# An attention transform that works in PSUM, shifted copies in parts, and another order for the stages beside it

## The chip, the cores and the metric

One core of a Trainium2 chip runs the whole program. The metric is the device time of one execution in microseconds (us). Before the change the median of three executions is 7252.11 us (7241.76 to 7254.39). The profiled execution has a span of 7245.1 us at a mean granted TensorE clock of 0.845.

## What is computed

Two layers on four images `x[4, 96, 128, 128]`, all in float32. Layer 0 is a selective-scan block; it isn't touched except for its last step, which is called norm here: layer norm over 192 channels, a projection to 96 channels and the residual. Layer 1, which the change concerns, is for each image:

```python
# xr, x1, x2: a "split norm" of the group-normed image: parts above and below the mean
x1 = sc1 * relu(x) + x1n;   x2 = sc2 * (x - relu(x)) + x2n
key, qry = unfold(conv2d(x1, aw1), 3), unfold(conv2d(x2, aw2), 3)
attn = softmax(einsum('bckl,bqkl->bqck', key, qry) / sqrt(C * 9))      # [96, 96 * 9]
value = conv2d(x1, aw3)
y1 = layer_norm(conv2d(value, attn as 3x3 weights))
y2 = layer_norm(conv2d(x2, w_conv2)) * x1
out = x + xr + conv1x1(concat(y1, y2), w_full) + b_full
```

All 3x3 convolutions have 96 channels in and out.

## The kernel before

**Convolution as products.** The columns of a row are cut in tiles of four. A tile with its borders (six columns) is turned into six planes by sums and differences (`planes_of`, L1319 and on); the convolution is then six products with transformed weights (`products`, L1371 on), and an output transform makes four columns of the six results (`outputs`, L1438 on). The planes of x1, x2 and value lie in DRAM (`x1p`, `x2p`, `vp`).

`planes_of` has two forms. `at_once` does all on VectorE. `scaled` makes scaled copies x4 and x2 on ScalarE (L1346, L1347), and `differences` makes the planes from them on GpSimd (L1352 to L1358, in the profile df, x and pl).

`products` works on a strip of 12 rows. It takes three pairs of PSUM banks (tile `two`): one pair for products 0 and 5, one for 1 and 3 ("a"), one for 2 and 4 ("b"). Each product sums three matrix products, from `ya` (planes as loaded), from `yb` (the first 64 channels of ya shifted by one and two rows, L1393 both) and from the last 32 channels (L1408). `yb` is made by ScalarE in `turn` (L1797), in two copies of 64x2376, before the products of the strip ahead. `outputs` copies the first pair to SBUF (`ou`, L1456) and pair a (`sd`, L1480) on ScalarE; VectorE makes sums and differences of pair a with pair b (L1464, L1465), adds to `ou` (L1466), and writes the four columns with L1474, each from two SBUF tiles.

**Attention** of one image (`attention`): for each of 11 strips and each of two maps (x1 and x2), one set of products of 128 channels and one of 64 channels on two half strips; beside these the transposes and products that make the attention map (`taps`, L1655 and L1551). Then softmax, and 11 more strips of products over value (`vp`). Image 0 has only these last 11, since its first part is done in another way ahead of this (`direct_maps`, L1948).

**Light work beside it.** `norm` (`ssm_output`, L942 to L1041) makes layer 0's output. `split` (`split_norm`) has a first pass for statistics (L1093 to L1100) and a second pass that makes x1 and x2 (L1196 on ScalarE, L1201 on VectorE, tile `half`) and their planes, 16 pieces of 8 rows with two sides each. `close` (`attn_output`, L2060 to L2076) joins all to the output.

**Order.** All work is written as generators that yield a cost. `co_run` lets the light generator go on as far as the attention generator (left) has paid; when left ends, what is left of light is drained. `Later` holds work back for a number of ticks, so that evacuations are issued between products. An instruction scheduler then orders each engine's queue; a queue runs in order, and DMAs from SP have one queue. The light work goes round in this way (stage b is attention of image b):

```python
    for b in range(NB):
        after = []
        if 0 < b and b + 1 < NB:
            after.append(imgs[b + 1].split(psr, "right"))
        if b:
            imgs[b].begin()
            after.append(imgs[b - 1].close(psr, "right"))
        if b + 2 < NB:
            imgs[b + 2] = Image(b + 2)
            after.append(imgs[b + 2].norm(yms[b // 2 + 1][b % 2], psr, "right"))
        light = chain(*([light] if b == 0 else []), *after)
```

The `light` of stage 0 is what remains of norm and split of image 1. The attention pool `psa` has three pairs of PSUM banks, `psr`, for light work, has two single banks.

## Time and profile before

| Stretch, us | What runs | Length |
|---|---|---|
| 3740 to 3945 | stage 0: image 0's value products, second pass of split of image 1 | 205 |
| 3945 to 4012 | stage 0: rest of that split | 67 |
| 4012 to 4262 | stage 0: norm of image 2 | 250 |
| 4262 to 5370 | stage 1: attention of image 1, with split of image 2 (to 4850), close of image 0 (to 5045), norm of image 3 | 1108 |
| 5370 to 6375 | stage 2: attention of image 2, with split of image 3 (to 5975), close of image 1 (to 6180), then nothing | 1005 |
| 6375 to 7110 | stage 3: attention of image 3, with close of image 2 (to 6585), then nothing | 735 |
| 7110 to 7245 | close of image 3 | 135 |

Before 3740 us lie layer 0's projection and scan and image 0's first part. Over the whole span PE is busy 76%, VectorE 68%, ScalarE 53% and GpSimd 52%; these are means over stages with different limits, so the stages have to be read one by one. In the profile PE is TensorE's matmul, PEld its weight load, DVE is VectorE, ACT ScalarE, POOL GpSimd, and SP the engine that issues most DMAs. In a group of instructions the tile before the arrow is written, those behind it are read; then come the count, the busy time, the mean of one in ns, and the idle time before it with what ended it.

### The profile page before, as it was taken

How to read it: one execution, taken by the hardware profiler on the slowest of the kernel's cores; microseconds unless marked ns; L12 is line 12 of the kernel's file. 1: busy time of each engine (PE TensorE's matmuls, PEld its weight loads, DVE VectorE, ACT ScalarE, POOL GpSimd, SP SyncE). 2: the span in 40 equal slices, each digit the busy share in tenths (PEclk: the TensorE clock that was granted, in tenths of full speed). 3: DMA queues.
4: the chain of work that ended last, by engine and by line, in shares of the span. 5: the costliest groups of instructions: out<-in, count | busy, mean ns of one | idle time of the engine just before them, and what ended most of it. 6: DMA issues, size and time to landing. Idle time of an engine off the chain costs nothing. (4 is left out here: it accounts for less than half of the span.)

```text
span 7245.1 us, 74140 instructions
## 1 busy us (share of the span) xinstructions
PE 5487.0 (76%) x23256; PEld 2382.5 (33%) x23256; DVE 4907.5 (68%) x6580; ACT 3876.0 (53%) x4296; POOL 3731.4 (52%) x2734
## 2 busy tenths in 40 slices
PE   5889989878877289999834565568875668888887
PEld 2333323222221044443311123334333334445542
DVE  3257779888975788895478346558566558676457
ACT  1357677777865766773333254444455444444443
POOL 2237669788874388892123228972217982122310
PEclk9999989989976599999867577779887779889887
DMA  8767777757666667567665553447674436665346
GB/s 145 183 155 192 200 196 211 224 162 211 186 166 187 183 197 218 173 189 190 177 164 155 136 141 98 111 111 186 167 184 105 111 101 178 152 176 131 91 120 171
DMA packets 886276, 1183.96 MB, mean 163 GB/s; under 512 B 208190, under 2 KB 745350, under 8 KB 873404
## 3 DMA queue, kind: packets, MB, share of 16 engines
q1 hardware_dynamic: 862268, 1124.28, 59.1%
q0 software_dynamic: 16208, 38.42, 2.0%
q10 hardware_dynamic: 7408, 16.53, 0.8%
q8 instruction: 186, 3.05, 0.2%
q14 instruction: 206, 1.69, 0.1%
HBM read 771.50 MB, written 337.56 MB: 153 GB/s over the span
## 5 line engine op out<-in xcount | busy, mean ns | idle before, releaser
L621 PE MATMUL bank<-y,wp 128*128 128x512 f32 (+3 forms) x3584 | 1315.4, 623 | 94.9 <-DVE z L497 39.9
L854 POOL TENSOR_TENSOR y<-y,dl 128x1024 f32<-128x1024 f32 x384 | 1057.7, 2754 | 267.4 <-DVE dl L846 233.3
L821 POOL TENSOR_TENSOR dl<-dl,u 128x1024 f32<-128x1024 f32 x384 | 1012.9, 2638 | 223.2 <-ACT dA L797 102.7
L842 DVE TENSOR_TENSOR_SCAN dA<-dA,pBC 128x512 f32<-128x512 f32 x768 | 981.6, 1278 | 30.7
L1393 PE MATMUL two<-ya,wd 128*64 128x192 f32 (+3 forms) x2376 | 622.3, 446 | 330.7 <-ACT sd L1480 219.1
L621 PEld LDWEIGHTS bank<-y,wp 128*128 128x128 f32 (+3 forms) x3584 | 458.6, 169 | 763.2 <-issue 653.0
L1948 PE MATMUL bank<-y,wn 128*128 128x384 f32 (+5 forms) x2408 | 676.4, 504 | 41.6 <-DMA y<-x2d 16.6
L846 DVE TENSOR_TENSOR dl<-dA,pBC 128x512 f32<-128x512 f32 x768 | 528.7, 688 | 262.6 <-PE pBC L735 189.0
L735 PE MATMUL pBC<-xr,wbc 60*128 60x512 bf16 (+1 forms) x1536 | 456.9, 402 | 329.1 <-DVE dA L842 256.1
L1393 PE MATMUL two<-yb,wd 128*64 128x192 f32 (+3 forms) x2376 | 594.2, 427 | 3.7 <-ACT yb L1797 3.7
L664 ACT ACTIVATE dl<-pd,dtb 128x512 f32<-128x512 f32 x768 | 486.2, 684 | 186.9 <-PE pd L735 173.7
L1464 DVE TENSOR_TENSOR sd<-sd,two 128x384 f32<-128x384 f32 (+5 forms) x176 | 137.6, 782 | 586.9 <-ACT sd L1480 577.9
L1797 ACT COPY yb<-ya 64x2376 f32<-64x2376 f32 (+1 forms) x220 | 468.1, 2128 | 123.5 <-DMA ya<-vp 61.3
L825 DVE TENSOR_TENSOR pBC<-dl,pBC 128x512 f32<-128x512 f32 x768 | 527.5, 687 | 8.0 <-POOL dl L821 7.0
L1393 PEld LDWEIGHTS two<-ya,wd 128*64 128x64 f32 (+1 forms) x2376 | 283.6, 180 | 536.5 <-ACT sd L1480 231.4
L797 ACT ACTIVATE dA<-dl,negA 128x1024 f32<-128x1024 f32 x384 | 420.3, 1141 | 2.3
L1948 PEld LDWEIGHTS bank<-y,wn 128*128 128x128 f32 (+3 forms) x2408 | 309.1, 168 | 340.0 <-issue 177.4
L1352 POOL TENSOR_TENSOR df<-own,x 96x792 f32<-96x792 f32 (+1 forms) x66 | 208.6, 3161 | 372.9 <-ACT x L1346 372.2
L949 PE MATMUL bank<-y,mean 96*32 96x512 f32 x512 | 256.3, 793 | 168.7 <-DMA y<-yms 101.7
L1393 PEld LDWEIGHTS two<-yb,wd 128*64 128x64 f32 (+1 forms) x2376 | 311.4, 180 | 170.9 <-issue 51.2
L664 ACT ACT_TABLE_LOAD x245 | 314.3, 1283 | 96.5 <-PE pd L735 89.3
L1201 DVE SCALAR_TENSOR_TENSOR half<-xn,kept,half 96x1024 f32<-96x1024 f32 x128 | 215.4, 1697 | 210.5 <-ACT half L1196 177.2
(303 smaller groups left out, 10293.8 us busy)
## 6 DMA issues: line engine op xcount, KB each, us to landing
u<-zb SPq DMA_DIRECT2D x192, 1024.0 KB
yms<-y SPq DMA_DIRECT2D x96, 512.0 KB
y<-yms SPq DMA_DIRECT2D x64, 768.0 KB
xn<-xnew SPq DMA_DIRECT2D x128, 384.0 KB
ya<-vp SPq DMA_DIRECT2D x40, 1039.5 KB
y<-y SPq DMA_DIRECT2D x128, 258.2 KB
zb<-z SPq DMA_DIRECT2D x64, 512.0 KB
ya<-x1p SPq DMA_DIRECT2D x30, 1039.5 KB
```

The costliest lines, as they stand in the source:

```text
L621: nc.tensor.matmul(blocks(pz[p:e]), lhsT=ws[k][:, d, c : c + e - p], rhs=window(ys[k], at, d, n), start=(i == 0), stop=(i == len(terms) - 1),)
L664: nc.scalar.activation(dst, src, AF.Softplus, bias=bias)
L735: nc.tensor.matmul(p, lhsT=w[rows], rhs=xr[rows, at : at + CH], start=True, stop=True)
L797: nc.scalar.activation(live[m]["dA"], live[m]["dl"], AF.Exp, scale=negA[:, g % 3, k : k + 1])
L821: nc.gpsimd.tensor_mul(t, t, u_view(n))
L825: nc.vector.tensor_mul(p, live[n]["dl"][:, bass.ts(half, CH)], p)
L842: nc.vector.tensor_tensor_scan(h, h, p, init, ALU.mult, ALU.add)
L846: nc.vector.tensor_mul(live[n]["dl"][:, sl], live[n]["dA"][:, sl], live[n]["C", half])
L854: nc.gpsimd.tensor_add(v, v, t.rearrange("p (a b) -> p a b", b=W))
L1393: nc.tensor.matmul(of(to[p:e], r), lhsT=w[:, i, c : c + e - p], rhs=tiles(t[k][:, i], o, r), start=(k == 0), stop=False,)
L1797: nc.scalar.copy(yb[64 * h - 64 : 64 * h, :, :n], ya[0:64, :, h * PT : h * PT + n])
L1948: nc.tensor.matmul(pc[p:e, :n].rearrange("p (h w) -> p h w", w=W), lhsT=w[:, c : c + e - p], rhs=v[:, :, 0:W], start=(i == 0), stop=(i == ...
```

## The change

1. **Output transform.** ScalarE copies the first pair (`ends`) and the half pair a (`odd`) to SBUF as before. VectorE makes sums and differences so that one operand of every instruction stays in PSUM: the results for pair b are written over pair b itself, the others to a tile `wide` in SBUF. So the four column writes read one SBUF and one PSUM operand. The same is done in split's second pass: ScalarE's scaled input goes to a PSUM bank, in two parts of 512 for each side, and not to `half`. It is for freeing VectorE and GpSimd of their competition for SBUF.
2. **Shifted copies in parts.** `turn` gives six copies of two planes and 64 channels each, which `products` issues one by one behind its products (`beside`).
3. **Buffers and order in the planes.** x4 and x2 have two buffers where the planes have two, `half` has two in place of three, and GpSimd writes the planes that need x2 first.
4. **Stages.** In stage b from 1 on, the light work is norm of image b + 1, split of image b + 1, close of image b − 1. Stage 0 keeps only what remains of image 1.

```diff
--- before
+++ after
@@ -1181,3 +1181,3 @@
             if planes:
-                half = [dict(name="half", bufs=3)] * 2
+                half = [dict(name="half")] * 2
             for i in range(NS):
@@ -1195,10 +1195,14 @@
                         to = hv[:, :, 1:PW]
-                    nc.scalar.activation(
-                        to, v, AF.Identity,
-                        scale=scale[:, side_ : side_ + 1], bias=shift[:, side_ : side_ + 1],
-                    )
                     op = ALU.is_le if side_ else ALU.is_gt
-                    later(lambda to=to, v=v, op=op: nc.vector.scalar_tensor_tensor(
-                        to, v, thr, to, op, ALU.mult
-                    ))
+                    for a in range(0, RS, R) if planes else (0,):
+                        r = R if planes else RS
+                        x, o = v[:, a : a + r], to[:, a : a + r]
+                        f = part(ps, C, R, W) if planes else o
+                        nc.scalar.activation(
+                            f, x, AF.Identity,
+                            scale=scale[:, side_ : side_ + 1], bias=shift[:, side_ : side_ + 1],
+                        )
+                        later(lambda o=o, x=x, f=f, op=op: nc.vector.scalar_tensor_tensor(
+                            o, x, thr, f, op, ALU.mult
+                        ))
                     later(stored(i, m, h), 1 + 3 * side_ * planes)
@@ -1343,4 +1347,4 @@
         def scaled():
-            x4 = pool.tile([C, most * PP], F32, name="x4", bufs=1)[:, : r * PP]
-            x2 = tile("x2", 2, 1)
+            x4 = pool.tile([C, most * PP], F32, name="x4", bufs=bufs)[:, : r * PP]
+            x2 = tile("x2", 2, bufs)
             nc.scalar.mul(x4, t[:, : r * PP], a2)
@@ -1354,6 +1358,6 @@
             nc.gpsimd.tensor_sub(x2[:, 1], by_k(t, 4)[:, 0], by_k(t, 2)[:, 0])
-            nc.gpsimd.tensor_sub(pl[:, 0:NP:5], f[:, 2:4], f[:, 0:2])
-            for i, x in ((1, f[:, 1:3]), (3, x2)):
+            for i, x in ((3, x2), (1, f[:, 1:3])):
                 nc.gpsimd.tensor_add(pl[:, i], x[:, 1], x[:, 0])
                 nc.gpsimd.tensor_sub(pl[:, i + 1], x[:, 1], x[:, 0])
+            nc.gpsimd.tensor_sub(pl[:, 0:NP:5], f[:, 2:4], f[:, 0:2])
             later(lambda: then(pl), 2)
@@ -1370,3 +1374,3 @@
 
-    def products(ps, jobs, ws, later, evac, threes=False):
+    def products(ps, jobs, ws, later, evac, threes=False, fill=()):
 
@@ -1416,2 +1420,9 @@
         outer, sums = evac
+        fill = iter(fill)
+
+        def beside():
+            for f in (next(fill, None),):
+                if f:
+                    f()
+
         a = pairs_of(ps)
@@ -1420,2 +1431,3 @@
             main(to[i], i)
+            beside()
             later.tick()
@@ -1430,2 +1442,3 @@
             main(to[i], i)
+            beside()
             later.tick()
@@ -1450,27 +1463,28 @@
 
-        def outer(c):
-            def copied():
-                t = pool.tile([128, 2, 2, AR * TN], F32, name="sd", bufs=1)
-                u = pool.tile([128, 2, AR * TN], F32, name="ou")
-                got.extend((t[:m, :, :, :n], u[:m, :, :n]))
-                nc.scalar.copy(got[1], c[:m, :, :n])
+        def copy_of(x, name, bufs):
+            t = pool.tile([128, 2, AR * TN], F32, name=name, bufs=bufs)[:m, :, :n]
+            nc.scalar.copy(t, x[:m, :, :n])
+            return t
 
-            later(copied)
+        def outer(c):
+            later(lambda: got.append(copy_of(c, "ends", 2)))
 
         def sums(a, b):
-            def combined():
-                s, d = got[0][:, 0], got[0][:, 1]
-                u = got[1]
-                nc.vector.tensor_sub(d, s, b[:m, :, :n])
-                nc.vector.tensor_add(s, s, b[:m, :, :n])
-                nc.vector.tensor_add(u, u, got[0][:, :, 0])
-                for p, e, v in parts:
-                    for k, x, f, y in (
-                        (0, s[p:e, 1], 1.0, u[p:e, 0]),
-                        (1, d[p:e, 1], AA, d[p:e, 0]),
-                        (2, s[p:e, 1], AA * AA, s[p:e, 0]),
-                        (3, d[p:e, 1], AA * AA * AA, u[p:e, 1]),
-                    ):
+            def first():
+                t = copy_of(a, "odd", 1)
+                later(lambda: combined(t))
+
+            def combined(t):
+                w = pool.tile([128, 2, AR * TN], F32, name="wide", bufs=1)[:m, :, :n]
+                ends, v = got[0], b[:m, :, :n]
+                nc.vector.tensor_sub(w[:, 1], t[:, 1], v[:, 1])
+                nc.vector.tensor_add(w[:, 0], t[:, 1], v[:, 1])
+                nc.vector.tensor_sub(v[:, 1], t[:, 0], v[:, 0])
+                nc.vector.tensor_add(v[:, 0], t[:, 0], v[:, 0])
+                for k, j, f in ((1, 1, AA), (2, 0, AA * AA), (0, 0, 1.0), (3, 1, AA**3)):
+                    if k == 0:
+                        nc.vector.tensor_add(v, ends, v)
+                    for p, e, o in parts:
                         nc.vector.scalar_tensor_tensor(
-                            at(v, k), rows(x), f, rows(y), ALU.mult, ALU.add
+                            at(o, k), rows(w[p:e, j]), f, rows(v[p:e, j]), ALU.mult, ALU.add
                         )
@@ -1478,6 +1492,2 @@
 
-            def first():
-                nc.scalar.copy(got[0][:, 0], a[:m, :, :n])
-                later(combined)
-
             later(first)
@@ -1791,11 +1801,20 @@
             def turn(c):
-                if c < len(todo):
-                    n = (todo[c][1][1] + 2) // 3 * 3 * PT
-                    ya, yc = raw.pop(c)
-                    yb = p2.tile([128, NP, AR * PT], F32, name="yb")
-                    for h in (1, 2):
-                        nc.scalar.copy(
-                            yb[64 * h - 64 : 64 * h, :, :n], ya[0:64, :, h * PT : h * PT + n]
-                        )
-                    cols[c] = ya, yb, yc
+
+                if c >= len(todo):
+                    return []
+                n = (todo[c][1][1] + 2) // 3 * 3 * PT
+                ya, yc = raw.pop(c)
+                yb = p2.tile([128, NP, AR * PT], F32, name="yb")
+                cols[c] = ya, yb, yc
+
+                def copy(h, i):
+                    nc.scalar.copy(
+                        yb[64 * h - 64 : 64 * h, i, :n], ya[0:64, i, h * PT : h * PT + n]
+                    )
+
+                return [
+                    lambda h=h, i=i: copy(h, i)
+                    for i in (slice(0, NP, 5), slice(1, 4, 2), slice(2, 5, 2))
+                    for h in (1, 2)
+                ]
 
@@ -1803,3 +1822,4 @@
             load(1)
-            turn(0)
+            for f in turn(0):
+                f()
             c = 0
@@ -1827,3 +1847,3 @@
                     for m in (0, 1):
-                        turn(c + 1)
+                        fill = turn(c + 1)
                         t = cols.pop(c)
@@ -1849,3 +1869,4 @@
                         yield from products(
-                            ps, [(0, 128, 0, t, 0, r3)], pairs[m], later, evac, True
+                            ps, [(0, 128, 0, t, 0, r3)], pairs[m], later, evac, True,
+                            [None, None] + fill[:4],
                         )
@@ -1876,3 +1897,3 @@
                         evac = outputs(p2, 128, hr * TN, to, later, then)
-                        yield from products(ps, jobs, pairs[m], later, evac)
+                        yield from products(ps, jobs, pairs[m], later, evac, fill=fill[4:])
                         load(c + 2)
@@ -1887,3 +1908,3 @@
             for i, (r0, r) in enumerate(chunks):
-                turn(c + 1)
+                fill = turn(c + 1)
                 t = cols.pop(c)
@@ -1900,3 +1921,3 @@
                 evac = outputs(p2, C, r * TN, to, later, out)
-                yield from products(ps, [(0, C, 0, t, 0, r)], ws, later, evac)
+                yield from products(ps, [(0, C, 0, t, 0, r)], ws, later, evac, fill=fill)
                 load(c + 2)
@@ -2206,11 +2227,10 @@
         after = []
-        if 0 < b and b + 1 < NB:
-            after.append(imgs[b + 1].split(psr, "right"))
         if b:
             imgs[b].begin()
+            if b + 1 < NB:
+                imgs[b + 1] = Image(b + 1)
+                after.append(imgs[b + 1].norm(yms[(b + 1) // 2][(b + 1) % 2], psr, "right"))
+                after.append(imgs[b + 1].split(psr, "right"))
             after.append(imgs[b - 1].close(psr, "right"))
-        if b + 2 < NB:
-            imgs[b + 2] = Image(b + 2)
-            after.append(imgs[b + 2].norm(yms[b // 2 + 1][b % 2], psr, "right"))
-        light = chain(*([light] if b == 0 else []), *after)
+        light = chain(*([] if b else [light]), *after)
         left = imgs[b].attend(psl)
```

## The prediction

> **What bounds the kernel now.** I read the page's 40 slices first. Up to about 3640 us the diff touches little, so I read only the part after it, in the table of busy time by stretch. I chose the cuts where a line's instructions begin or end (L942 marks a norm, L1201 a second pass of a split, L2074 a close). Columns: length, then busy time of PE, weight load, VectorE, ScalarE and GpSimd, granted clock, DMA share, GB/s.
>
> ```profile
> core 0: us, PE busy (x) PEld busy (x) DVE busy (x) ACT busy (x) POOL busy (x), PEclk, DMA share, GB/s
> 4012.00:4262.00 250.00, 167.35 (x384) 37.78 (x384) 77.11 (x136) 65.31 (x80) 56.79 (x64) 0.62 0.50 136
> 4320.00:4850.00 530.00, 312.83 (x1868) 195.08 (x1866) 320.95 (x352) 261.29 (x259) 453.07 (x450) 0.75 0.42 108
> 5045.00:5370.00 325.00, 290.43 (x1213) 117.83 (x1212) 191.66 (x317) 152.43 (x154) 72.45 (x84) 0.89 0.70 181
> 5445.00:5975.00 530.00, 309.71 (x1828) 193.24 (x1830) 311.62 (x340) 257.64 (x252) 450.76 (x448) 0.75 0.42 106
> 6180.00:6375.00 195.00, 156.96 (x769) 82.17 (x763) 124.09 (x191) 88.89 (x74) 17.24 (x20) 0.88 0.61 151
> 6585.00:6980.00 395.00, 330.60 (x2340) 218.05 (x2340) 198.32 (x339) 185.67 (x179) 115.67 (x129) 0.88 0.41 99
> ```
>
> First row: the norm of image 2 runs alone for 250 us; no attention product stands beside it, and the PE clock is at 0.62. Third row: the norm of image 3, beside the end of image 1's attention. Rows 2 and 4: the second pass of split for images 2 and 3; GpSimd is busy 85%, PE 59%, so GpSimd sets these 530 us. Row 5: the end of image 2's attention with nothing beside it. Last row: image 3's attention alone, set by no engine but by a loop (below).
>
> Next, inside row 2, the groups of VectorE instructions (busy, mean ns | idle before) and the waits (total us, times, longest).
>
> ```profile
> L1201 DVE SCALAR_TENSOR_TENSOR half<-xn,kept,half 96x1024 f32<-96x1024 f32 x32 | 62.5, 1957 | 96.3 <-ACT half L1196 75.2 <-POOL x L1353 13.8 <-POOL x L1354 7.2
> L1474 DVE SCALAR_TENSOR_TENSOR ring<-sd 128x384 f32<-128x384 f32 x28 | 47.0, 1679 | 0.0
> L1464 DVE TENSOR_TENSOR sd<-sd,two 128x768 f32<-128x768 f32 x14 | 13.3, 952 | 67.6 <-ACT sd L1480 67.6
> ```
>
> ```profile
> POOL x L1353 <- ACT x L1347: 33.7, 5, 7.2
> POOL half L1314 <- ACT xz L1100: 17.1, 1, 17.1
> POOL df L1352 <- ACT x L1346: 13.3, 1, 13.3
> ACT x L1347 <- POOL pl L1358: 94.3, 22, 9.4
> ACT x L1346 <- POOL df L1352: 86.4, 27, 8.0
> ACT half L1196 <- POOL x L1354: 40.3, 21, 6.2
> PE two L1393 <- ACT sd L1480: 78.9, 11, 15.1
> PE two L1655 <- ACT ou L1456: 50.9, 9, 13.7
> ```
>
> L1474 and L1201 read two SBUF tiles and take 1679 and 1957 ns; the same shapes take 830 to 880 ns in stretches without GpSimd and 1257 ns at the least. L1464 reads one operand from PSUM and stays at 952 ns. ScalarE stands 221 us in its queue behind GpSimd (94.3 + 86.4 + 40.3), and PE then waits for ScalarE's copies.
>
> Last, the timeline of image 3's attention.
>
> ```profile
> 6697.14 4.36 ACT L1797 COPY yb<-ya 64x2376 f32<-64x2376 f32 x2 [2.23 <-DMA ya<-x2p]
> 6701.52 0.80 ACT L1480 COPY sd<-two 128x768 f32<-128x768 f32 x1
> 6702.36 0.95 DVE L1464 TENSOR_TENSOR sd<-sd,two 128x768 f32<-128x768 f32 x1 [8.37 <-ACT sd L1480]
> 6702.38 1.52 PE L1655 MATMUL two<-ident,ring 96*85 96x96 f32 x10 [0.73 <-ACT sd L1480]
> ```
>
> The last product of the strip before ended at 6689.0; the load into its ya landed at 6697.1; two shifted copies hold ScalarE for 4.4 us; only then is the PSUM pair copied out.
>
> **What the skill says.** The Trainium skill, SBUF — State Buffer, section "Who interferes with whom": a VectorE instruction with two SBUF inputs contends with a GpSimd instruction that reads SBUF, and the later one waits; with at most one SBUF input it does not. The trace agrees (1679 against 952 ns above). Vector Engine (DVE) Microarchitecture Reference, 5.2: a destination that hops every element costs 1.7 to 2.5 ns per column instead of 1.04. The trace agrees: L1474, which writes every fourth word, takes about 850 ns for 384 columns, 2.2 ns each; moving a source to PSUM leaves that as it is. Perfetto Trace Analysis, "Matmuls": matmul groups should rotate through PSUM banks so that evacuation overlaps; here three pairs rotate, and the change holds one of them longer.
>
> **The change part by part.**
>
> *Order of norm, split, close.* Beside image 0's attention the norm of image 2 goes; it moves to image 1's attention, where the norm of image 3 goes out to image 2's. By their yields a norm costs 150 units, a split 278, a close 83, an attention 503. Stage 1 has 150 + 278 + 83 = 511 units before and after. Stage 0 loses its 250 us. Stage 2 grows from 361 to 511 units: the 142 units of attention that run alone now (195 us, row 5) get a norm beside them. Row 3 shows what such a pair costs: 325 us, and as the norm is 150 units of which 142 fit, I take 320. So +320 − 195 = +125, and the sum is −250 + 125 = **−125 us**. Ends: if PE were the only limit, the pair would take about 235 us (the norm's 167 us at clock 0.62 is some 110 at 0.92, plus about 125 for the products), giving −210; if close beside the value products at the end of stage 1 stretches their loads by 40 us, −85.
>
> *PSUM operands and doubled buffers in the split stages.* GpSimd's own times without contention, from the shortest and median rows: a side of a piece 4.14 + 0.74 + 0.65 + 1.29 + 4 × 0.74 + 0.33 (memsets) = 10.1 us, 32 of them 323 us; a value half-strip 3.13 + 0.53 + 0.53 + 1.01 + 4 × 0.53 = 7.3 us, 12 of them 88 us. That is 411 us against 453 busy. Idle now is 77 us: 47 wait for x4 and x2, which two buffers remove, and about 20 stand at the start and stay. I leave 25 us for imperfect filling: 411 + 20 + 25 = 456, so −74 for each of two images, **−148 us**. VectorE falls with it, but lies beside GpSimd and counts nothing by itself. New cost, hidden: L1201 becomes four instructions of 512 with PSUM, at 746 ns (L2074's mean, same kind) 2.98 us a piece against 3.9; ScalarE's four of about 0.68 us (L664) are 2.7 against 2.5 us. New wait: only two psr banks, so the third ScalarE part waits for VectorE, and queued behind it are the copies that free attention's PSUM pairs, so PE waits too. VectorE's queue there is at most one transform, 6.6 us, once per piece; GpSimd has a second x4 and x2 by then. I take zero, and 74 us an image as the bad end. `half` with two buffers instead of three costs nothing: L1354, the last reader, ends 4 us before the batch does.
>
> *The same in stage 0.* Split of image 1 until 4012 is set by VectorE (167 of 205 us busy). Its L1201 changes little, the transform loses contention: **−10 us**.
>
> *Output transform, elsewhere.* Before: 3 × 0.95 + 4 × 0.85 = 6.25 us per 128x768 product; after: 4 × 0.55 + 0.95 + 4 × 0.85 = 6.55. No PSUM-to-strided row exists; between 0.85 (the store sets it) and 0.95 I take 0.85. But pair b is free only after the last of these: 6.55 us after the copy of pair a, against 1.9. Waiting for it are the next products; of three pairs the first is free after its 0.8 us copy, so a transpose or the next outer pair can use it. In the loop above PE needs pair b about 5 us after the copy, and by then the outer pair is free again. I cost it at nothing; bad end: 2 to 2.6 us per product.
>
> *Shifted copies in six parts.* L1797 takes 2172 ns for 64x2376 and 1679 ns for 64x1782, so 0.83 ns an element and 0.20 us fixed: 64x792 takes 0.86 us, six make 5.2 against 4.35 us of ScalarE, which is half idle. The copy of pair a waits for four parts (3.0 us, as back-to-back starts overlap) instead of 4.4: about 1.2 us less per strip and map. For 22 in image 3 and a few elsewhere, **−30 us**.
>
> Sum: −125 − 148 − 10 − 30 = −313; 7252 − 313 = **6939, say 6940 us**.
>
> **The rivals.**
> 1. *GpSimd stages stay at 530 us*, because the wait on two psr banks takes the place of the wait on x4. For it: ScalarE runs in order and its 221 us of waits show how it blocks. Against: GpSimd's idle lines name x4 and x2 only. 7252 − 125 − 40 = 7087, say 7090.
> 2. *Slower: pair b held too long.* The wait becomes 4.6 us longer per product; outside the split stages there are about 176 (L1464's count) − 50 = 126 products. If 2.6 us of it stays visible: +328. With −125 for the order and −150 of the rest: 7252 + 53 = 7305. For it: PE's waits for L1480 show that pairs are short. Against: the outer pair frees early.
> 3. *The norm hides better*, −200 in place of −125, and the split stages reach 435 us (−190): 7252 − 200 − 190 − 20 = 6842, say 6840.
>
> **How the numbers follow.** First case 0.50, rival 1 0.25, rival 2 0.10, rival 3 0.15. The range 6830 to 7110 takes in the first case, rival 1 and the better part of rival 3, and leaves out rival 2 and the rest, under 2 in 10. Faster: 0.50 + 0.25 + 0.15 less 0.02 for a bad mix of the ends, 0.88; same 0.02; slower 0.10.
>
> **What would show it.** Order: L942 and products (L1393) stand in the same stretches of stages 1 and 2, at 16 to 18 us a step of the norm. Contention: L1474's mean for 128x384 below 0.95 us in the split stages and L1352 near 4.15 us. Buffers: GpSimd's waits for L1346 and L1347 near zero there, its busy share over 90%. Pair b: PE's waits for L1474's successor lines small; if they pass 100 us in image 3's attention, rival 2 is right. It would be wrong above all if ScalarE's queue, not GpSimd, sets the split stages, or if close beside the value products runs slower than the norm did.

## The result and the profile after

The changed kernel takes **7037 us** in the median (7019.15 to 7040.78), beside 7248.5 us for the kernel before: ratio 0.970 [0.968, 0.972], 211 us less. The forecast was 6940 us with a range of 6830 to 7110: right side, inside the range, but 97 us of the expected gain are missing.

To find them I cut each profiled execution where the loads of the next image's attention begin (the first load of `ya` from `x1p`), and, for stage 3, at the tenth of the eleven stores of `od` (an image's value strips end in these stores). The column "forecast" sorts the prediction's own terms by stage.

| Part | before | after | change | forecast |
|---|---|---|---|---|
| up to the start of stage 1 | 4264.1 | 4001.2 | −263 | −260 |
| stage 1 | 1105.2 | 1055.7 | −50 | −74 |
| stage 2 | 1006.1 | 1061.5 | +55 | +125 − 74 = +51 |
| stage 3 up to the tenth value store | 734.8 | 765.9 | **+31** | −30 |
| last strip and last close | 134.9 | 133.0 | −2 | 0 |

The profiled execution of the changed kernel is the fastest of its four, 7019 us, so the changes in this table add to −228 us and not to −211: 85 of the 313 us are missing in it. Three kernels below that are the same as the changed one up to the start of stage 1 reach it at 4012, 4011 and 3984 us, so the first row is good to some 10 us only. Two rows fit within 5 us. Most of what is missing lies in stage 3, whose own work changed only in the output transform and the shifted copies. The stretches of the changed kernel (columns: from, to, length, then busy time of PE, weight load, VectorE, ScalarE and GpSimd with counts, granted clock, DMA share, GB/s):

```profile
core 0: us, PE busy (x) PEld busy (x) DVE busy (x) ACT busy (x) POOL busy (x), PEclk, DMA share, GB/s
4005.00:4300.00 295.00, 262.65 (x1452) 120.35 (x1453) 168.65 (x296) 159.29 (x198) 112.37 (x126) 0.93 0.67 169
4385.00:4840.00 455.00, 280.17 (x1738) 181.10 (x1736) 198.77 (x370) 247.36 (x301) 383.52 (x436) 0.75 0.43 108
4840.00:5075.00 235.00, 188.19 (x560) 77.09 (x561) 194.34 (x254) 113.28 (x127) 8.87 (x12) 0.86 0.83 216
...
5450.00:5890.00 440.00, 264.92 (x1644) 170.45 (x1644) 185.29 (x336) 239.72 (x290) 376.15 (x428) 0.76 0.43 109
...
6345.00:6745.00 400.00, 338.76 (x2329) 219.92 (x2330) 214.19 (x394) 191.69 (x238) 111.22 (x129) 0.88 0.39 94
```

Row 1 is the norm of image 2, now beside attention products: 295 us, in the place of 250 us alone in stage 0. Rows 2 and 4 lie in the second passes of split. Their 455 and 440 us can't be set against the 530 of before: those windows began 28 us ahead of the pass's first instruction (4348 and 5473 us), row 2 begins 6 us ahead of it (4391), and row 4 ends 17 us before the last planes are stored (5907). Bounded as the windows of before, the changed kernel's stretches are 490 and 492 us (4363 to 4853, 5419 to 5911). From the first to the last store of planes the pass takes 442 and 444 us, before 483 and 483. Row 3 is the close of image 0, now beside the value products. From its first load of `o` to its last store of `out` that close takes 204 us, where it took 199 beside map products. The last row is image 3's attention alone, 400 us and no better than the 395 of before.

Groups of instructions inside row 2 (busy, mean ns | idle before them, and what ended it):

```profile
L1356 POOL TENSOR_TENSOR df<-half,x 96x1056 f32<-96x1056 f32 x32 | 132.8, 4149 | 16.1 <-DVE half L1205 15.3
L1205 DVE SCALAR_TENSOR_TENSOR half<-xn,kept,bank 96x512 f32<-96x512 f32 x64 | 47.1, 740 | 162.6 <-POOL df L1356 125.1 <-POOL x L1358 35.5 <-ACT bank L1201 2.0
L1488 DVE SCALAR_TENSOR_TENSOR ring<-wide,two 128x384 f32<-128x384 f32 x40 | 31.6, 866 | 0.5
L1361 POOL TENSOR_TENSOR pl<-df 96x264 f32<-96x264 f32 x31 | 23.0, 743 | 0.0
L1360 POOL TENSOR_TENSOR pl<-df 96x264 f32<-96x264 f32 x31 | 23.0, 741 | 0.0
```

The competition is gone. The column write is at 866 ns beside GpSimd (L1474 before: 1679), the multiply at 2 × 740 ns a side (L1201 before: 1957). GpSimd's own instructions are at the undisturbed times that the prediction took for them (4.14 and 0.74 us). The waits in the same stretch (total us, times, longest):

```profile
DVE half L1205 <- POOL df L1356: 125.1, 21, 19.3
ACT bank L1201 <- DVE half L1205: 100.6, 24, 7.1
PE two L1397 <- ACT odd L1466: 57.1, 7, 16.8
...
PE two L1665 <- DVE oc L1488: 28.6, 5, 14.8
...
POOL pl L1360 <- DMA x2p<-pl: 22.5, 3, 9.4
...
POOL x L1357 <- ACT x L1351: 15.7, 7, 3.0
POOL df L1356 <- DVE half L1205: 15.3, 1, 15.3
```

GpSimd is no longer kept waiting by x4 and x2 (16 us). The wait for the last reader of `half` has moved to VectorE, and ScalarE now waits for the two PSUM banks, as the forecast feared. Of GpSimd's 71.5 idle us, 31.6 are now waits for stores that give `pl` back (22.5 for those to `x2p`; in the window of before 5.7 in all). PE waits for VectorE's column writes, 55 us in all over this window (28.6 for `oc`), where it waited 1.4 us for VectorE's sums before: the longer hold of pair b shows here, while GpSimd is the busiest engine.

Last, the timeline of image 3's attention; the lines answer those of before.

```profile
6553.32 0.80 ACT L1466 COPY ends<-two 128x768 f32<-128x768 f32 x1 [5.83 <-DVE two L1486]
...
6556.80 5.17 ACT L1811 COPY yb<-ya 64x792 f32<-64x792 f32 x6 [2.68 <-DMA ya<-x2p]
...
6561.99 0.80 ACT L1466 COPY odd<-two 128x768 f32<-128x768 f32 x1
6562.82 0.56 DVE L1480 TENSOR_TENSOR wide<-odd,two 128x384 f32<-128x384 f32 x1 [7.58 <-ACT odd L1466]
6562.84 1.41 PE L1665 MATMUL two<-ident,ring 96*85 96x96 f32 x10 [1.99 <-ACT odd L1466]
```

The six parts of the shifted copy don't lie between the products. They run as one block of 5.2 us as soon as their load is in, and the copy of pair a (`odd`) stands behind all six. Before, that block was two copies of 4.4 us together. One strip (two maps) takes 49.9 us here, as the mean of five strips without light work, and 48.5 before.

### The profile page after: what moved, and what is told of

Read it like the earlier page. It is cut to its first block, busy times and chain, and to the rows that moved or that the text cites. A ratio compares the mean times of both kernels' runs of the same rounds, so it can differ in the third digit from the quotient of the medians.

```text
span 7017.3 us, 75070 instructions
## 1 busy us (share of the span) xinstructions
PE 5401.3 (77%) x23256; PEld 2362.9 (34%) x23256; DVE 4776.1 (68%) x7028; ACT 3974.0 (57%) x4832; POOL 3557.3 (51%) x2734
## 5 line engine op out<-in xcount | busy, mean ns | idle before, releaser
L1811 ACT COPY yb<-ya 64x792 f32<-64x792 f32 (+1 forms) x660 | 551.5, 836 | 171.6 <-DMA ya<-x1p 56.2
L1480 DVE TENSOR_TENSOR wide<-odd,two 128x192 f32<-128x192 f32 (+5 forms) x176 | 81.7, 464 | 496.9 <-ACT odd L1466 481.3
L1205 DVE SCALAR_TENSOR_TENSOR half<-xn,kept,bank 96x512 f32<-96x512 f32 x192 | 140.3, 741 | 342.7 <-POOL df L1356 250.1
L735 PEld LDWEIGHTS <-wbc 60*128 60x128 bf16 (+1 forms) x1536 | 103.3, 96 | 766.4 <-issue 752.7
L1397 PE MATMUL two<-ya,wa 128*96 128x384 f32 (+1 forms) x528 | 232.1, 523 | 162.3 <-DVE mrows L2222 84.6
```

Of the source, the lines that this page charges most:

```text
L735: nc.tensor.matmul(p, lhsT=w[rows], rhs=xr[rows, at : at + CH], start=True, stop=True)
L1397: nc.tensor.matmul(of(to[p:e], r), lhsT=w[:, i, c : c + e - p], rhs=tiles(t[k][:, i], o, r), start=(k == 0), stop=False,)
L1811: nc.scalar.copy(yb[64 * h - 64 : 64 * h, i, :n], ya[0:64, i, h * PT : h * PT + n])
```

## Experiments: one part undone at a time

In these five, one part of the changed kernel is put back as it was.

**Order of the stages.**

```diff
+        if 0 < b and b + 1 < NB:
+            after.append(imgs[b + 1].split(psr, "right"))
         if b:
             imgs[b].begin()
...
-                after.append(imgs[b + 1].norm(...))
-                after.append(imgs[b + 1].split(psr, "right"))
             after.append(imgs[b - 1].close(psr, "right"))
...
+        if b + 2 < NB:
...
+            after.append(imgs[b + 2].norm(...))
...
```

> The changed kernel (7037 us) with the order of norm, split and close as before. Theory (prediction): the order is worth 125 us, so about 7160; the norm of image 2 stands alone again for about 250 us, and the end of image 2's attention runs alone again for about 195 us. Rival: beside the faster split stages the order is worth little more than half of that, because close now stretches the value products: about 7100.

Measured 7113.12 us, ratio 0.983 [0.980, 0.985]: 76 us slower than the changed kernel. By stages: up to stage 1 +230, stage 2 −121 (forecast −125), stage 1 +2, stage 3 −20 (746.4 us). The last isn't scatter: the changed kernel and the four below that share its attention and have norm and split moved as it has (close first, and the three with less close) take 762 to 769 us for it. In the old order the light work of stage 2 has ended before the cut, and the first loads for the close of image 2 are issued 18 us ahead of it. In the new order the close of image 1 stores until 3 us after the cut, and those loads follow 10 us after it. So stage 3 starts with more of its light work still to do. That this costs the 20 us was not tested by itself.

**Shifted copies** in two instructions of 64x2376 at `turn`, ahead of the strip.

```diff
-                def copy(h, i):
+                for h in (1, 2):
                     nc.scalar.copy(
-                        yb[64 * h - 64 : 64 * h, i, :n], ya[0:64, i, h * PT : h * PT + n]
+                        yb[64 * h - 64 : 64 * h, :, :n], ya[0:64, :, h * PT : h * PT + n]
                     )
...
-                return [...]
+                return []
```

> The changed kernel with the shifted copies in two whole copies ahead of the products, as before. Theory (prediction): the parts save 1.2 us per strip and map, so this is slower by 30: about 7067. Rival: the six parts run as one block of 5.2 us in place of 4.36 us ahead of the copy of pair a, and cost time: faster by 20 to 40, about 7005; in image 3's attention alone a strip and map then takes 23 to 24 us in place of 25.0.

Measured 7069.5 us, ratio 0.977 [0.975, 0.979]: the parts are worth 32 us, the size that was forecast, but not where it was forecast. In the profiles stages 1 and 2 lose 32 and 27 us without them; stage 3 *gains* 19 (746.8 us; a strip of image 3 takes 47.0 us). (The profiles differ by 48 us, 16 more than the medians, as that of the changed kernel is its fastest execution.) In stage 1 the eleven value strips beside close take 186 us from first to last store against 170. There ScalarE's queue also carries close's activations; that this is the reason wasn't tested.

**Output transform** as before (copies `sd` and `ou`, sums in SBUF).

```diff
-                t = copy_of(a, "odd", 1)
...
-                w = pool.tile([128, 2, AR * TN], F32, name="wide", bufs=1)[:m, :, :n]
...
-                nc.vector.tensor_sub(v[:, 1], t[:, 0], v[:, 0])
...
+                nc.vector.tensor_sub(d, s, b[:m, :, :n])
+                nc.vector.tensor_add(s, s, b[:m, :, :n])
```

> The changed kernel with the output transform of before (two SBUF operands, pair b free after two VectorE instructions). Theory (prediction): contention returns in the two split stages at some 40 us each and 10 us in stage 0, and nothing is gained elsewhere: about 7130; L1352's successor goes from 4149 to about 4300 ns. Rival (pair b is held too long): outside the split stages a strip and map gets 2 us shorter, which gives back 70 us: about 7060, with image 3's attention alone at 23 us per strip and map.

Measured 7074.2 us, ratio 0.977 [0.975, 0.979]: worth 37 us. From first to last store of planes a split takes 467 us (442 in the changed kernel, 483 before).

**x4 and x2** with one buffer, and the differences in the old order.

```diff
-            x4 = pool.tile([C, most * PP], F32, name="x4", bufs=bufs)[:, : r * PP]
-            x2 = tile("x2", 2, bufs)
+            x4 = pool.tile([C, most * PP], F32, name="x4", bufs=1)[:, : r * PP]
+            x2 = tile("x2", 2, 1)
...
```

> The changed kernel with x4 and x2 in one buffer each and the order of the differences as before. Theory (prediction): GpSimd's waits for x4 and x2 return with 47 us in each split stage: about 7130, and ScalarE waits for GpSimd again (about 180 us per stage). Rival: without contention GpSimd is fast enough that these waits are short, and the DMA of the planes ends the wait: plus 20, about 7057.

Measured 7029.35 us, ratio 0.971 [0.968, 0.973]: the second buffers and the new order of the differences, undone together, are worth nothing. Some waits in the first split stretch of that kernel:

```profile
ACT x L1351 <- POOL pl L1362: 92.0, 28, 5.8
ACT x L1350 <- POOL df L1356: 71.6, 27, 7.9
POOL pl L1359 <- DMA x2p<-pl: 29.6, 4, 11.1
ACT bank L1201 <- DVE half L1205: 16.6, 16, 4.0
POOL pl L1359 <- DMA x1p<-pl: 10.7, 2, 9.5
POOL x L1357 <- ACT x L1351: 7.7, 3, 5.4
```

ScalarE waits 164 us for GpSimd to give x4 and x2 back, but its wait for the banks falls from 100.6 to 16.6: one wait stands where the other stood. GpSimd hardly feels it: it waits 11.8 us for x4 and x2 in all, and 41.5 for stores of the planes, as this experiment's rival had it. It is busy for 383.8 of 455 us, as with two buffers (383.5).

**f in SBUF** in the second pass of split. Three buffers of `half`, as before, have no room beside the rest, so this kernel has two.

```diff
-                    for a in range(0, RS, R) if planes else (0,):
...
-                        f = part(ps, C, R, W) if planes else o
-                        nc.scalar.activation(f, x, AF.Identity, ...)
...
+                    nc.scalar.activation(to, v, AF.Identity, ...)
+                    later(lambda to=to, v=v, op=op: nc.vector.scalar_tensor_tensor(
+                        to, v, thr, to, op, ALU.mult
+                    ))
```

> The changed kernel with one part undone: in the second pass of split, ScalarE writes f into the SBUF tile half again (one instruction of 1024) and VectorE multiplies there, with two buffers of half. Theory A (contention and queue): the multiply has two SBUF operands again, so it stands in the way of GpSimd (VectorE's mean goes from 0.74 us per 512 columns back to about 1.9 us per 1024) and the stretch in which the planes are stored goes from 442 us to about 460 us each; two images make about +40 us, so some 7077 us. Rival B (the wait on two PSUM banks, 100 us of ScalarE in one such stretch, costs what the contention gave): without that wait the stretch gets no longer, 435 to 445 us, and the time stays between 7010 and 7040 us. Rival C (two buffers of half instead of three now bind): ScalarE waits for GpSimd's last reader of half and the stretch goes past 480 us, above 7110 us.

Measured 7107.8 us, ratio 0.981 [0.979, 0.983]: worth 71 us, more than theory A and in time just short of rival C, and the planes' stretch is 471 us. Waits in that stretch:

```profile
DVE half L1201 <- ACT half L1196: 133.6, 23, 9.0
ACT half L1196 <- POOL df L1352: 118.5, 17, 10.7
PE two L1393 <- ACT odd L1462: 67.4, 9, 13.9
PE two L1393 <- ACT ends L1462: 58.1, 7, 12.8
ACT half L1196 <- POOL x L1354: 45.2, 7, 8.6
```

With f in a PSUM bank, the instruction that writes `half` is VectorE's; with f in `half`, it is ScalarE's, and ScalarE waits 164 us for GpSimd's last reads, with the copies of the PSUM pairs behind it. So part of the 71 us is probably this queue and not the ports. How much, I can't say from this run, since three buffers were not tried.

## Experiments: where the parts meet

**Both SBUF operands back** (the last two edits on transform and f together).

> The changed kernel with both parts undone that take an SBUF operand away from VectorE: f in half in SBUF, and the old output transform with its SBUF copies. The old transform alone cost +37 us. Theory A (the two are additive): +37 and what f alone costs, so near 7110 us if that is +40. Theory B (the whole contention of the split stages comes back only when both are gone, since each alone leaves slack): the planes' stretch is back at 483 us as before, about 41 us for each of two images, and 7120 to 7135 us. Rival C (contention isn't what set these stages, the doubled x4 and x2 did it): the stretch stays near 442 us and the time below 7090 us.

Measured 7149.58 us, ratio 0.987 [0.985, 0.988]: 112 us, near 37 + 71. Theory A, additive. The planes' stretch is 494 us. The groups show the competition back in full (window 4425 to 4950):

```profile
L1201 DVE SCALAR_TENSOR_TENSOR half<-xn,kept,half 96x1024 f32<-96x1024 f32 x32 | 56.2, 1761 | 119.7 <-ACT half L1196 119.6
L1483 DVE SCALAR_TENSOR_TENSOR ring<-sd 128x384 f32<-128x384 f32 x20 | 39.5, 1977 | 0.0
L1356 POOL TENSOR_TENSOR pl<-df 96x264 f32<-96x264 f32 x32 | 32.6, 1019 | 0.0
L1357 POOL TENSOR_TENSOR pl<-df 96x264 f32<-96x264 f32 x32 | 30.0, 937 | 0.0
```

What GpSimd pays doesn't grow with the columns of its instruction: 264 columns take 1019 and 937 ns here against 741 and 743 in the changed kernel, some 0.2 to 0.3 us more, while the 1056-column one goes only from 4149 to 4269. These are means over all such instructions, whether VectorE stood beside them or not.

**The order alone**, in the kernel before.

```diff
             imgs[b].begin()
+            if b + 1 < NB:
...
+                after.append(imgs[b + 1].norm(...))
+                after.append(imgs[b + 1].split(psr, "right"))
             after.append(imgs[b - 1].close(psr, "right"))
-        if b + 2 < NB:
...
-            after.append(imgs[b + 2].norm(...))
...
```

> The kernel before with one part of the change alone: norm, split and close in the new order. The prediction took -125 us for it (norm alone 250 us gone, 125 us more in stage 2), so 7123 us. Undoing the order in the changed kernel cost 76 us, so if the parts don't meet, -76 us and 7172 us. If close, which now stands beside value products instead of map products, is what takes the difference and does so in any kernel, 7165 to 7180 us; if the slower products of the changed kernel do, nearer 7123 us.

Measured 7155.22 us, ratio 0.987 [0.985, 0.988]: −89 us. In the profiles, which differ by 100 us: up to stage 1 −237, stage 2 +121, stage 1 +13, stage 3 and the last close +3. So the whole is, in steps: before 7244; order alone 7155; order with parts and buffers (and `half` with two) 7150, which can't be told from it; the PSUM operands on top, 7037. The five single undos, 76 + 32 + 37 + 71 − 8, make 208 of 211 us. But the 32 us of the parts don't show in the step from 7155 to 7150. `half` with two buffers, which ScalarE waits for where f lies in SBUF, may have taken them; no run separates the two.

**Close before norm and split**, so that it stands beside map products again.

```diff
             imgs[b].begin()
+            after.append(imgs[b - 1].close(psr, "right"))
             if b + 1 < NB:
...
                 after.append(imgs[b + 1].norm(...))
                 after.append(imgs[b + 1].split(psr, "right"))
-            after.append(imgs[b - 1].close(psr, "right"))
```

> The changed kernel with another order of the same parts beside the attention of image b: close of image b-1, then norm of b+1, then split of b+1. Theory A (close beside the value products takes 235 us where the same products took 195 us alone and the map products have room for it; each is held by DMA there, at 0.83 of the queues): close now stands beside map products and is hidden, split ends beside the value products, and each of stages 1 and 2 gets 20 to 40 us shorter; 6960 to 7000 us. Rival B (the attention products and the other work are a fixed sum of ScalarE and PE time, and what stands beside what does not matter): 7030 to 7045 us. Rival C (split's writes of planes then meet the loads of the value products): slower than 7060 us.

Measured 7052.6 us, ratio 0.974 [0.972, 0.976]. Theory A misses: stages 1 and 2 take 1064 and 1078 us against 1056 and 1061. The value products take 118 us from first to last store in stage 1 and not 170, but split now stands beside them, and its planes' stretch is 464 us and not 442. From the start of stage 1 to the first store of planes, close, norm and split's first pass take 599 us, where norm and that pass took 406: 193 us for close, against some 208 beside the value products (from the last store of planes to the end of the stage). So close is only 15 us shorter beside map products, and split loses 22.

## Experiments: what sets close beside the value products

The 235 us that the expectations start from are a window's length; the stretch itself, from the last store of planes to the end of the stage, is 208 us. Each kernel leaves out work of the close of images 0 and 1.

```diff
+                if img.b > 1:
-                nc.vector.scalar_tensor_tensor(e, xx, low[:, 0:1], e, ALU.mult, ALU.add)
+                    nc.vector.scalar_tensor_tensor(e, xx, low[:, 0:1], e, ALU.mult, ALU.add)
```

> The changed kernel with one of close's six VectorE instructions of each 1024 columns left out for images 0 and 1, the sum of xx times low (so these images' output lacks that term). It takes 16 x 1.28 = 20 us of VectorE from each of two stretches in which close stands beside the value products; there VectorE is busy 179 of 205 us and the DMA queues are at 0.83. Theory A (VectorE sets these stretches): each gets 15 to 20 us shorter, 7000 to 7010 us. Rival B (the transfers set them, as the prediction's bad end had it): 7030 to 7040 us.

```diff
+                if img.b > 1 or t % 4 == 3:
-                nc.sync.dma_start(ob[:, bass.ts(t, SN)], e)
+                    nc.sync.dma_start(ob[:, bass.ts(t, SN)], e)
```

> The changed kernel with three of four stores of the output left out for images 0 and 1: 4.7 MB less in each of the two stretches in which close stands beside the value products, of some 48 MB. Theory A (VectorE sets these stretches): no change, 7025 to 7040 us. Rival B (the transfers set them): a tenth of 235 us for each of two, so some 6990 to 7000 us.

```diff
+                    if img.b > 1:
-                    nc.tensor.matmul(pf, lhsT=w1, rhs=o[:, sl], start=True, stop=False)
-                    nc.tensor.matmul(pf, lhsT=w2, rhs=c2[:, sl], start=False, stop=True)
+                        nc.tensor.matmul(pf, lhsT=w1, rhs=o[:, sl], start=True, stop=False)
+                    nc.tensor.matmul(pf, lhsT=w2, rhs=c2[:, sl], start=img.b < 2, stop=True)
```

> The changed kernel with one of close's two matrix products of each 512 columns left out for images 0 and 1, the one over o (so these images' output lacks that term; the load of o stays). It takes 64 records or 34 us of PE from each of two stretches in which close stands beside the value products. Neither 20 us of VectorE nor a tenth of the transfers moved those. Theory A (PE's work adds up there: eleven value strips take 101 us alone and 170 us beside close, and close is 72 us of PE): each stretch gets 25 to 34 us shorter, 6970 to 6990 us. Rival B (the chain from load to x, c and the product sets the pace of close, and the value products keep step with it): 7025 to 7040 us.

| Left out | us (its before) | ratio | stages 1, 2 |
|---|---|---|---|
| nothing (changed kernel) | 7037.13 (7248.5) | 0.970 [0.968, 0.972] | 1056, 1061 |
| 20 us of VectorE | 7032.31 (7242.03) | 0.971 [0.969, 0.973] | 1056, 1066 |
| 4.7 MB of stores | 7025.32 (7242.03) | 0.970 [0.968, 0.973] | 1060, 1061 |
| 34 us of PE (estimate) | 6999.96 (7209.16) | 0.970 [0.968, 0.973] | 1059, 1064 |

The last run and the kernel before beside it were both some 35 us faster than in the other rows, so the ratio and the stages count; neither moves. A window of 205 us in the stretch in question, in the changed kernel, then without the VectorE work, then without the PE work:

```profile
4845.00:5050.00 205.00, 173.22 (x530) 70.83 (x531) 179.26 (x236) 105.42 (x117) 3.90 (x5) 0.91 0.83 219
```

```profile
4857.00:5062.00 205.00, 171.11 (x528) 70.26 (x529) 161.56 (x223) 102.91 (x115) 4.20 (x6) 0.92 0.83 220
```

```profile
4831.00:5036.00 205.00, 152.27 (x471) 63.55 (x471) 180.49 (x240) 105.49 (x117) 4.37 (x6) 0.84 0.83 221
```

The work is really gone (VectorE 179 to 162, PE 173 to 152 us; without the stores the DMA share goes from 0.83 to 0.78), and the stretch is as long as before: from the last store of planes to the end of stage 1 it takes 208, 206, 209 and 207 us in the four kernels (changed; less VectorE, stores, PE). So none of VectorE, PE and a tenth of the transfers sets it alone. Whether they do in turn, or the chain of waits through the in-order queues does, stays open: leaving out two at once was not tried.

## Experiment: the parts behind the copy of pair a

In the emitted program all six parts now come beside the second product of a strip. As the instruction scheduler would still pull them forward once their load is in, each is also tied behind `odd` of the first product in ScalarE's queue, by an order without a semaphore.

```diff
-                            ps, [(0, 128, 0, t, 0, r3)], pairs[m], later, evac, True,
-                            [None, None] + fill[:4],
+                            ps, [(0, 128, 0, t, 0, r3)], pairs[m], later, evac, True
...
-                        yield from products(ps, jobs, pairs[m], later, evac, fill=fill[4:])
+                        yield from products(ps, jobs, pairs[m], later, evac, fill=fill)
...
+                    if odds:
+                        behind(traced()[-1], odds[-1])
```

> The changed kernel, with the six parts of the shifted copy for the next strip issued beside the second product of the strip, and each held in ScalarE's queue behind the copy of pair a (odd) of the first product. In the changed kernel's image 3 alone, five or six parts stand in a block of 4.3 to 5.2 us ahead of odd, and PE waits for odd (32 and 18 us in 400 us). Theory A (that block is why stage 3 took 766 us and not 735 or less): odd follows ends by about 4 us, its wait is gone, and stage 3 up to the last value strip takes 735 to 745 us; with 20 to 30 us from there and little elsewhere, 7000 to 7020 us. Rival B (pair b, held by VectorE for 6.5 us, is what PE waits for; the copy's place doesn't matter): stage 3 stays above 755 us and the time within 15 us of 7037. Rival C (the parts now come too late for the next strip, whose first products need planes 0 and 5): slower than 7050 us.

Measured **6995.85 us**, ratio 0.966 [0.964, 0.969], the best of all. Stage 3 up to the tenth value store takes 722 us, 44 less than in the changed kernel and 13 less than before; stages 1 and 2 take 1059 and 1072. The timeline of ScalarE in image 3's attention:

```profile
6544.58 0.80 ACT L1479 COPY ends<-two 128x768 f32<-128x768 f32 x1 [4.60 <-DVE two L1501]
6550.88 0.80 ACT L1479 COPY odd<-two 128x768 f32<-128x768 f32 x1 [5.50 <-PE two L1425]
6551.57 2.58 ACT L1826 COPY yb<-ya 64x792 f32<-64x792 f32 x3
6556.08 1.72 ACT L1826 COPY yb<-ya 64x792 f32<-64x792 f32 x2
6559.34 0.85 ACT L1826 COPY yb<-ya 64x792 f32<-64x792 f32 x1
```

Now `odd` waits for PE, not for the load, and the parts fill gaps behind it. A strip takes 44.7 us in place of 49.9. What PE waits for in 395 us of the kernel before (6585 to 6980), then in 380 us of the changed kernel and of this one:

```profile
PE two L1655 <- ACT ou L1456: 35.4, 7, 6.4
PE two L1655 <- ACT sd L1480: 13.2, 7, 5.0
PE two L1393 <- ACT sd L1480: 4.1, 3, 2.9
```

```profile
PE two L1397 <- ACT odd L1466: 29.0, 8, 5.3
PE two L1665 <- ACT odd L1466: 18.5, 8, 2.9
PE two L1397 <- ACT kt L1670: 7.6, 7, 1.3
```

```profile
PE two L1410 <- ACT kt L1685: 29.0, 21, 4.8
...
PE two L1410 <- ACT odd L1479: 2.5, 1, 2.5
```

47.5 us of waiting for `odd` become 2.5; some of it comes back as waits for the copies `kt` (29 against 8). So in the changed kernel it is the block ahead of `odd` that PE waited for, not pair b. But PE waited as long in the kernel before: 52.7 us for `ou` and `sd`, as the block stood ahead of `ou` in one of the two maps (two copies from 6723.45, `ou` at 6727.82). The block alone therefore doesn't explain why the changed kernel's strips are slower than before. Stage 3 cut at the copies `ends` (`ou` before) of the 128-channel products, in us, for this kernel and for those above:

| Kernel | beside close (to the 9th copy) | five strips alone | to the first value copy | value |
|---|---|---|---|---|
| before | 268 | 242 | 110 | 115 |
| order alone | 278 | 241 | 110 | 114 |
| changed | 286 | 250 | 116 | 114 |
| changed, order undone | 271 | 246 | 115 | 115 |
| changed, shifted copies undone | 284 | 235 | 113 | 114 |
| changed, transform undone | 290 | 243 | 113 | 113 |
| changed, both SBUF operands back | 287 | 239 | 113 | 112 |
| parts behind `odd` | 276 | 224 | 107 | 116 |

Of the 31 us that stage 3 lost, 13 are in the two middle columns, where the attention runs without light work. The other 18 are beside the close of image 2, and most of them go with the order: 268 and 271 us in the two kernels with the old order, 276 to 290 in the others. The second column says more of the 13. Six parts with the old transform take 243 and 239 us, about as much as the 242 and 241 of the kernels with both parts as before; two copies with the new transform take 235; only both together take 246 and 250. Why they meet so is open: in these five strips PE waits 36.5 us in the changed kernel and 34.7 before, and its 1441 records are busy 212.7 and 207.7 us.

## Why the prediction came out as it did

**Order (−125 forecast, −89 alone, −76 undone).** The two large terms were right: −237 for −250, +121 for +125. Two smaller ones were missing. In stage 1 the prediction held 511 units before and after and so no change; with the order alone it is 13 us longer. Close went from map products to value products, the bad end that was named at 40 us, and from first load to last store it takes 218 us there and not 199; the norm beside map products takes 294 us from first to last instruction, where image 3's took 306 beside the end of the attention. And stage 3, for which the prediction held nothing from the order, takes 8 us more with the order alone, and 20 less in the changed kernel when the order is undone. The cause that was named for close, the loads of the value products, isn't shown: a tenth of the transfers less changed nothing.

**Split stages (−74 each forecast).** The window of 455 us seems to meet the forecast of 456, but with the bounds of the 530 us it is 490 and 492: 40 and 38 us came of 74. The step that failed is GpSimd's idle time. The prediction had 411 us busy and 45 idle; in the 490 us GpSimd works 392 and idles 98. (The 411 is a sum of single durations, and GpSimd's instructions overlap a little in the record.) Its test "busy over 90%" fails at 80%, or 84% in the window shown. The waits for stores of the planes alone, 32 us, are more than the 25 us left for imperfect filling; those for x4 and x2, which were to go, keep 16, and another 15 us are one wait for VectorE to write `half`. Of the two things that the step joined, the PSUM operands did it all (112 us over all stages, a part of it by the moved wait for `half`) and the doubled x4 and x2 nothing. The 47 us of GpSimd's waits that they were to remove shrink to 11.8 with one buffer as well; those waits named the tile that ScalarE was late with, not a buffer that was missing.

The contention itself is as the Trainium skill has it (SBUF — State Buffer, "Who interferes with whom": two SBUF inputs on VectorE contend with GpSimd's reads, at most one, outside the two-port modes, does not): the column write goes to 866 ns and `df` to 4149 ns, the "below 0.95" and "near 4.15" of the forecast.

**Stage 0 (−10 forecast).** Taking the PSUM operands away delays the start of stage 1 from 4001 to 4036 us. Of these 35, 17 stand before the first value store, 7 of them already at the start of image 1's norm, and scatter alone is some 10. The term was probably too small, and it made up for the 13 us missing from the order's first term: −263 for −260 is partly luck.

**Output transform elsewhere (0 forecast).** Rival 2's sign is absent: in image 3's attention PE waits 2.5 us for VectorE's column writes, far below 100. There pair b's longer hold is hidden: with `odd` in time stage 3 takes 722 us, less than the 735 with the old transform in the kernel before. In the split stage it isn't: PE waits 55 us for column writes there, and what that costs wasn't measured.

**Shifted copies (−30 forecast, −32 undone).** The size was right and the mechanism wrong. "The copy of pair a waits for four parts" failed: it waits for five or six, up to 5.2 us against 4.4, because the place of emission isn't the place in the queue. Nor do the parts overlap as was assumed: six take 5.17 us, 0.86 each, so four would take 3.4 us and not 3.0. The Trainium skill (Perfetto Trace Analysis, "Tensor Engine Instruction") calls ScalarE strict first-in, first-out; the trace agrees, `odd` starts 0.02 us after the block ends. The prediction also took the timeline of one map for both; in the other the block of before stood ahead of `ou`. So stage 3, which was to gain 30 us, lost 31. That is 61 of the 85 us missing in the profile: 43 in the strips without light work (−30 forecast, +13 measured; the parts and the new transform together, for a reason that stays open) and 18 beside close, of which 10 (order alone) to 15 (order undone) go with the order. The parts earn their 32 us in stages 1 and 2, where the forecast put "a few".

**Rivals.** Rival 1 (split stages stay as long) is out: some 40 us an image came, though not 74. The wait for two banks came, 100.6 us, and hurt no more than the wait whose place it took. Rival 3's better hiding of the norm didn't come. The whole lies between the likeliest case and rival 1 for reasons that neither named.

## What to carry to other kernels

A piece of work placed between two products in the program isn't there in the queue when a scheduler orders the queues: read the order in the timeline, and ask what stands ahead of the copy that frees PSUM when a load is late. A wait tells which tile was late, not which buffer to double: before adding one, see what the releasing engine was itself waiting for. And a forecast that fits in its sum can still be wrong in its terms: compare it stage by stage, between the same two events in both kernels, since a window cut by eye can carry work of its neighbour.

## What I had not expected of the hardware

- The contention costs GpSimd 0.1 to 0.3 us an instruction in the mean, and no more for a long one (741 to 1019 ns at 264 columns, 4149 to 4269 at 1056), so short instructions suffer most for their length; VectorE's column write goes from 866 ns with one PSUM operand to 1977 with two SBUF operands.
- Close beside value products keeps its length with VectorE, PE or the stores relieved one at a time, though VectorE is busy 87% and PE 84% there. High busy shares on two engines together don't name a bound. Leaving out two at once was not tried.
